# A Mamba block with a dequantized linear layer behind it: the first 512 tokens' x products in two steps of 256 tokens, out_proj's weights turned later

## Chip, cores and metric

The kernel runs on one core of one Trainium2 chip. The metric is the device time of one execution in microseconds, the median of several runs. The core has five engines, each with its own instruction stream: PE (matmul; its weight loads are listed apart as PEld), DVE (vector), ACT (scalar, activation functions), POOL (GpSimd) and SP (here it issues all DMAs). On-chip memory is SBUF (128 partitions) and PSUM (eight banks of 512 float32 a partition), into which PE writes.

## What is computed

For one sequence of L = 4096 tokens of width H = 1024 (float32):

```python
# inner width DIN = 2048, N = 16 states a channel, K = 4 taps, R = 64
def attn(hidden_states):                      # hidden_states = layernorm(x)
    proj = hidden_states @ in_proj_w          # 1024 -> 4096
    x, z = jnp.split(proj, 2, axis=-1)
    xc = conv_b + sum(conv_w[:, k] * shift(x, K - 1 - k))   # causal, along tokens
    xc = silu(xc)
    ssm_p = einsum('bdl,ed->ble', xc, x_proj_w)             # 2048 -> 64 + 16 + 16
    dt_r, Bm, Cm = rmsnorm of its three parts
    dt = softplus(einsum('blr,dr->bdl', dt_r, dt_proj_w) + dt_bias)
    A = -exp(A_log)
    # for every channel d and state n, token after token:
    #   h = exp(dt * A) * h + dt * B * xc ;  y = sum_n h * C
    y = (ys + D_param * xc) * silu(z)
    return einsum('bdl,hd->blh', y, out_proj_w)

x = x + attn(layernorm(x))
x = x + (layernorm(x) @ dequantized_W.T + bias)             # 1024 -> 1024
```

The recurrence over tokens is the scan: its state h carries from token to token, so the token steps go in order.

## The kernel before

**Steps.** Tokens are worked on in chunks of `TC` = 512 (`sizes`, L343), and the scan in steps of `TS` = 256 tokens. DIN is 16 tiles of 128 channels (`ND`), in four groups of four (`NG`). A `block` (L1121) is one scan step of one group; each has two halves (`hf`) of two channel tiles and eight pairs of states (`k`), so that the scan is 64 blocks of 16 units, 1024 units of 2 channel tiles x 2 states x 256 tokens.

**A unit.** `unit_b` (L965) makes `h = u * B` on POOL (L972) and puts the carried state's part into its first column (ACT, L974). `unit_e` (L976) makes `da = exp(dt * A)` on ACT into two PSUM tiles (L984). `unit_s` (L986) scans on DVE (L997), copies the last token's state on ACT into `state` (L1001) and multiplies by C: on DVE (L1003, when the scan's result lies in `da`) or on POOL (L1005, when it lies in `h`); which of the two is chosen unit by unit from the work counted so far. Eight transposes on PE (L1014) then add the products up in the PSUM tile `py`. `unit_b` runs three units ahead (`B_AHEAD`), `unit_e` one (`E_AHEAD`); there are 7 buffers for `h` and 4 for `da`. After eight pairs `py` is copied out (L1192) and `epilogue` (L937) transposes it, multiplies by silu(z), read back from DRAM, and stores y as two parts.

**Matrix products.** Float32 operands are split in a high and a low part, and `product` (L594) makes three matmuls for each of eight 128-row parts of the contraction (L610 to L612), so 24 to a tile. Weights come through `load_wi` (L622): at chunk 0 raw weights are loaded, split on chip, and the split parts stored to DRAM for later; the high half of an x weight is stored at chunk 1 (its low half at chunk 0), and later uses load the split parts (`load_w`). Each tile takes two of the four `w` buffers.

**Stages of a chunk.** `norm_transpose` (L522) normalizes rows and turns them. `gen_x` (L655) makes the 16 x tiles: product, convolution (ACT L685, three steps on DVE L688, last three tokens kept in `halo`, L689), silu (L647, each with a table load before and behind it), store of xc, and behind every four (or two) tiles an `x_proj` (L705, L714). `rms_norms` (L724) and `rms_transpose` (L746) follow; they set the mark `("x", c)`, which the first block of chunk c needs. z tiles come either from `gen_z` (L769, chunk 0) or mixed tile by tile with the x tiles (`mixed`, all later chunks). `prep_group` (L866) makes dt for a block.

**Background.** The scan's loop (L1165) is the backbone. All other work is a generator, `gen_all` (L1086), from which `pull` (L1129) takes a share after each unit: `total * (i + LEAD) / len(units)`. Before the loop it is pulled until the mark `("x", 0)` is there: this is the head of the kernel, without a scan. `side` holds small jobs (turning of weights) that are slipped into the products, `later` delays steps behind a product.

**Order on the engines.** `Order` records every instruction, gives it a rank (its place in the program, less a lead), and `schedule` (L204) replays all of them with a cost for each (`cost`, L161): each engine takes the ready instruction of lowest rank. The order that comes out is fixed with dependencies (`tie`, L304). The chip's engines then run their queues in that order. In the replay any two accesses to one PSUM tile depend on each other.

**Out_proj's weights.** `prep_out_w` (L474) loads out_proj's raw weights, turns them on PE, splits them on ACT and DVE and stores 32 pieces of 512 KB. It is a side job, put in behind `gen_z(0)` (L1088).

Of the kernel before, what the change touches and what calls it, by code (L numbers as in the profile page):

```python
# [16 lines left out]
F32 = mybir.dt.float32  # L17
# [3 lines left out]
ALU = mybir.AluOpType  # L21
# [4 lines left out]
P = 128  # L26
TC = 512
TS = 256
BIG = 1e28
LEAD = 20  # L30
PREP_N = 2
FIRST = 2000
EPI_N = 0
PRE = 3
X_DELAY = 2
# [12 lines left out]
class Order:  # L48
# [112 lines left out]
    def cost(self, r, e, n, silu):  # L161

        op = r.opcode
        if e == 0:
            name = str(r.outs[0])
            if "xps" in name:
                g = 223
            elif "float32r" in str(r.ins[0].dtype):
                g = 6 + 0.434 * n
            else:  # L170
                g = 0.85 * n
            return g, g + 164
        if e == 1:
            if op == "LoadActFuncSet":
                return 1300, 1300
            if op == "TensorCopy":
                d = 170 + 0.815 * n
            else:
                wide = sum(getattr(x, "bass_ap", None) is not None for x in r.ins) > 1
                d = 200 + 1.02 * n if wide else 195 + 0.84 * n  # L180
            if n < 32:
                return 95, 190
            if silu:
                d += 1400
            elif str(r.outs[0].bass_ap.space).endswith("PSUM"):
                return d - 56, d + 17
            return d - 100, d
        if e == 2:
            d = 180 + 2.15 * n
            if op == "TensorTensor" and "pow" in str(r.op):  # L190
                d = 400 + 157 * n
            return d - 40, d
        if e == 3:
            d = 140 + 1.05 * n
            if op == "BNStats":
                d = 676
# [132 lines left out]
def mamba_ffn_kernel(ctx, tc, hs, in_w, conv_w, conv_b, xp_w, dt_w, dt_b, a_log, d_par, out_w,  # L329
# [10 lines left out]
    NG = ND // 4  # L340
    NHB = H // P
    NTS = TS // P
    sizes = [TC] * (L // TC)  # L343
    osizes = [TC] * (L // TC - 1) + [TS] * 2
    starts = [sum(sizes[:i]) for i in range(len(sizes))]
    ostarts = [sum(osizes[:i]) for i in range(len(osizes))]
# [27 lines left out]
    def dense(name):  # L374
        return ps_d.tile([P, TC], F32, tag="dense", name=name)
# [175 lines left out]
    def start(kind, c):  # L551

        assert kind == "x" or writes[id(x1b_s[c])] == NHB
        src = hs[starts[c]:starts[c] + sizes[c], :] if kind == "x" else x1b_s[c]
        it = norm_transpose(src)
        norms[kind, c] = (next(it), it)
        side.insert(0, [1, itertools.islice(it, PRE)])
# [33 lines left out]
        while later:  # L591
            yield later.pop(0)[1]()

    def product(ps, w, act):  # L594

        for k in range(KT):
            if k == 4:
                for e in later:
                    e[0] -= 1
                for e in [e for e in later if e[0] <= 0]:  # L600
                    later.remove(e)
                    yield e[1]()
            if k == 2 and side:
                for _ in range(side[0][0]):
                    yield from side_step()
            while len(act) < KT:
                yield next(norm_it[id(act)])
            hi, lo = act[k]
            wk = w[k // 4]
            nc.tensor.matmul(ps, wk[:, 0, k % 4, :], hi, start=(k == 0), stop=False)  # L610
            nc.tensor.matmul(ps, wk[:, 0, k % 4, :], lo, start=False, stop=False)  # L611
            nc.tensor.matmul(ps, wk[:, 1, k % 4, :], hi, start=False, stop=(k == KT - 1))  # L612
            yield 3 * MM * hi.shape[-1] / TC
# [38 lines left out]
    ctx_c = [dict() for _ in range(NCH)]  # L652
    done_marks = set()

    def gen_x(c, mixed, nxt=None):  # L655

        t0, sz = starts[c], sizes[c]
        nt = sz // P
        act = yield from finish("x", c)
        ctx_c[c]["xn"] = act  # L660
        ssm = smp.tile([P, TC // P, E], F32, tag="ssm", name="ssm", bufs=1)[:, :nt]
        corr = smp.tile([P, ND, 3], F32, tag="corr", name="corr", bufs=1)
        part = smp.tile([P, ND, 3], F32, tag="part", name="part", bufs=1)
# [6 lines left out]
        for p in range(ND // nx):  # L670
# [3 lines left out]
            for i in range(4):  # L674
                j = i // 2 if mixed else i
                m = p * nx + j
                if mixed and i % 2:
                    yield from z_tile(c, m, act, pre[:, nx + j, :])
                    continue
                w = load_wi(c, m)  # L680
                ps = dense("ips")[:, :sz]
                yield from product(ps, w, act)
                with tc.high_priority(1000):
                    t = pre[:, j, :]
                    nc.scalar.activation(t, ps, AF.Identity, scale=cw[:, m, 3:4], bias=cb[:, m:m + 1])  # L685
                    for k in (2, 1, 0):
                        o = t[:, 3 - k:]
                        nc.vector.scalar_tensor_tensor(o, ps[:, 0:sz - 3 + k], cw[:, m, k:k + 1], o, ALU.mult, ALU.add)  # L688
                    nc.scalar.copy(halo[:, m, :], ps[:, sz - 3:sz])  # L689
# [4 lines left out]
            if mixed:  # L694
                nc.sync.dma_start(sz_s[c][g][:, h:h + nx, :], pre[:, nx:, :])
                done_marks.add(("z", c, g, h))
            later.append([(X_DELAY if p < ND // nx - 1 else X_DELAY_LAST) if c else 1, partial(first, c, x_proj, c, p * nx, nx, pre, ssm)])
        later.append([X_DELAY_LAST if c else 1, partial(first, c, rms_norms, c, ssm)])

    def first(c, f, *args):  # L700
# [65 lines left out]
        done_marks.add(("x", c))  # L766
        return 2 * nt * TP

    def gen_z(c):  # L769
        act = ctx_c[c].pop("xn")  # L770
        sz = sizes[c]
        for g in range(NG):
            pre = prep.tile([P, 4, TC], F32, tag="pre", name="prez")[:, :, :sz]
            for j in range(4):
                yield from z_tile(c, g * 4 + j, act, pre[:, j, :])
            silu(pre)
            nc.sync.dma_start(sz_s[c][g], pre)
            done_marks.add(("z", c, g, 2))

    def z_tile(c, m, act, dst):  # L780
        w = load_wi(c, ND + m)
        ps = dense("zps")[:, :sizes[c]]
        yield from product(ps, w, act)
        with tc.high_priority(1000):
            nc.scalar.copy(dst, ps)
# [200 lines left out]
    def unit_s(v, py):  # L986
# [7 lines left out]
        for n in range(2):  # L994
            flat = da[n].rearrange("p a b -> p (a b)")
            hflat = h[:, n].rearrange("p a b -> p (a b)")
            nc.vector.tensor_tensor_scan(hflat if on_pool else flat, flat, hflat, 0.0, ALU.mult, ALU.add)  # L997
        for n in range(2):
            last = (h[:, n] if on_pool else da[n])[:, :, TS - 1]
            if not (c == NCH - 1 and s == sizes[c] // TS - 1):  # L1000
                nc.scalar.copy(state[:, g0:g0 + 2, 2 * k + n], last)  # L1001
            if not on_pool:
                nc.vector.tensor_tensor(h[:, n], da[n], cb_[:, n], ALU.mult)  # L1003
        if on_pool:
            nc.gpsimd.tensor_tensor(h, h, cb_, ALU.mult)  # L1005
        hc = h
        terms = [(n, hc[:, n]) for n in range(2)]
        if k == 0:
# [220 lines left out]
```

## Time and profile before

| | |
|---|---|
| median of 3 runs | 4419.52 us (4413.35 to 4423.57) |
| profiled execution | 4422.55 us, span 4420.8 us |
| mean granted TensorE clock | 0.968 |
| DMA | 1066.39 MB, mean 241 GB/s |
| scans (L997) | 2048: 1166 into da, 882 into h |
| exps of da (L984) | 4096, 473 ns each, 1858.6 us |
| first multiply by B on POOL (L972) | 1024, 2388 ns each, 2423.9 us |
| multiply by C on POOL (L1005) | 441, 2396 ns each, 1055.4 us |
| state copies on ACT (L1001) | 1098 from da of 160 ns, 822 from h of 188 ns |
| table loads on ACT (L647, L648) | 64 and 64, 1283 ns each |
| out_proj's weights turned | 285 to 504 us |

How to read it: the busy time of an engine is the sum of the stretches in which it had an instruction at work; busy PE also holds pipelined matmuls whose ends are modelled. A line such as "ACT x <- DVE y: 10, 5, 3" in the list of waits says that ACT stood idle 10 us in all, 5 times, at most 3 us, ahead of x until DVE had done y. Each engine works off its own queue in order, so a wait holds up what is queued behind it. The chain of waits follows the work that ended last back to the start, and names at each step what it was released by.

### The profile page before, as it was taken

To read this page: it belongs to the slowest core of one execution; us is meant where nothing else is said; L and a number is where in the kernel's file an instruction comes from. 1 tells how busy PE (TensorE), PEld (TensorE's weight loads), DVE (VectorE), ACT (ScalarE), POOL (GpSimd) and SP (SyncE) were. 2 spreads that over 40 slices of the span, in tenths; PEclk is the share of its full clock that TensorE was granted. 3 is DMA by queue.
4 is the path that set the end of the run, shared out by engine and by line. 5 is a ranking of instruction groups with operands and counts; after the bars stand their busy time and mean duration, and the time that the engine had idled before them with its cause. 6 is when DMAs were issued, how large, how long until landed. Compare 5 with 4: busy or idle time off the path is not lost.

```text
span 4420.8 us, 73712 instructions
## 1 busy us (share of the span) xinstructions
PE 4072.3 (92%) x23658; PEld 3451.4 (78%) x23658; DVE 3908.0 (88%) x4842; ACT 3573.4 (81%) x9854; POOL 3853.4 (87%) x2234
## 2 busy tenths in 40 slices
PE   8988899999988999999999999999999999998887
PEld 6767778777876887788777888788877878887776
DVE  5588889998999989999899999999989999998882
ACT  5788888888887888888888789888888877877671
POOL 0678799899997999999999999999998999999791
PEclk9989999999999999999999999999999999999987
DMA  8868866567678765987568875788566898988765
GB/s 261 270 226 286 289 215 217 178 201 222 187 249 273 238 216 174 298 263 246 180 209 272 254 255 184 250 277 277 189 200 215 302 320 264 308 256 275 241 223 189
DMA packets 693843, 1066.39 MB, mean 241 GB/s; under 512 B 63816, under 2 KB 488832, under 8 KB 692432
## 3 DMA queue, kind: packets, MB, share of 16 engines
q1 hardware_dynamic: 693456, 1061.68, 74.1%
q8 instruction: 187, 3.06, 0.3%
q14 instruction: 200, 1.64, 0.1%
HBM read 815.85 MB, written 245.63 MB: 240 GB/s over the span
## 4 chain that ended last, share of the span: by engine, by line
PE 47%; ACT 13%; POOL 13%; DVE 10%; DMA 8%; issue 4%; SPq 1%; DVEq 0%; POOLq 0%; ACTq 0%
PE py L1014 11%; POOL h L972 7%; ACT da L984 4%; DVE da L997 4%; POOL h L1005 4%; PE ops L610 3%; PE ops L611 3%; PE ops L612 3%; PE ips L610 3%; PE ips L612 3%; PE ips L611 3%; PE zps L610 2%; PE zps L611 2%; PE zps L612 2%; DVE h L1003 2%
## 5 line engine op out<-in xcount | busy, mean ns | idle before, releaser
L972 POOL TENSOR_TENSOR h<-xl,bb 128x1020 f32<-128x1020 f32 x1024 | 2423.9, 2388 | 214.7 <-PE py L1014 201.5
L984 ACT ACTIVATE da<-dt,amat 128x256 f32<-128x256 f32 x4096 | 1858.6, 473 | 186.0 <-DVE h L1003 143.4
L997 DVE TENSOR_TENSOR_SCAN da<-da,h 128x512 f32<-128x512 f32 x1166 | 1378.4, 1213 | 66.0 <-POOL h L972 26.5
L1014 PE MATMUL py<-ident,h 128*128 128x128 f32 x8192 | 1116.6, 280 | 97.9 <-POOL h L1005 73.7
L1014 PEld LDWEIGHTS py<-ident,h 128*128 128x128 f32 x8192 | 972.2, 144 | 219.2 <-POOL h L1005 103.1
L1005 POOL TENSOR_TENSOR h<-h,cc 128x1024 f32<-128x1024 f32 x441 | 1055.4, 2396 | 80.8 <-ACT state L1001 71.6
L997 DVE TENSOR_TENSOR_SCAN h<-da,h 128x512 f32<-128x512 f32 x882 | 1044.9, 1208 | 44.4 <-ACT da L984 32.5
L1003 DVE TENSOR_TENSOR h<-da,cc 128x512 f32<-128x512 f32 x1166 | 755.4, 677 | 49.0 <-ACT state L1001 48.0
L610 PE MATMUL ops<-yh,wt 128*128 128x512 f32 (+1 forms) x1152 | 457.2, 398 | 19.5 <-DMA yh<-y 5.8
L611 PE MATMUL ops<-yh,wt 128*128 128x512 f32 (+1 forms) x1152 | 431.4, 375 | 2.4 <-DMA yh<-y 2.2
L612 PE MATMUL ops<-yh,wt 128*128 128x512 f32 (+1 forms) x1152 | 431.0, 374 | 0.0
L610 PE MATMUL zps<-nh,wt 128*128 128x512 f32 x896 | 365.9, 408 | 6.9 <-DVE nh L409 2.8
L612 PE MATMUL zps<-nh,wt 128*128 128x512 f32 x896 | 358.4, 400 | 0.0
L611 PE MATMUL zps<-nh,wt 128*128 128x512 f32 x896 | 357.9, 399 | 0.0
L610 PE MATMUL ips<-nh,wt 128*128 128x512 f32 x768 | 316.1, 412 | 20.2 <-DVE ssm L721 8.4
L688 DVE SCALAR_TENSOR_TENSOR pre<-ips,cw,pre 128x511 f32<-128x511 f32 (+2 forms) x384 | 281.3, 733 | 48.6 <-ACT pre L685 41.6
L612 PE MATMUL ips<-nh,wt 128*128 128x512 f32 x768 | 307.2, 400 | 0.0
L611 PE MATMUL ips<-nh,wt 128*128 128x512 f32 x768 | 306.7, 399 | 0.0
L1001 ACT COPY state<-da 128x2 f32<-128x2 f32 x1098 | 158.8, 160 | 150.0 <-DVE da L997 144.5
L610 PEld LDWEIGHTS ops<-yh,wt 128*128 128x128 f32 x1152 | 223.0, 194 | 53.0 <-DVE xb L835 7.7
L612 PEld LDWEIGHTS ops<-yh,wt 128*128 128x128 f32 x1152 | 222.0, 193 | 36.4
L611 PEld LDWEIGHTS ops<-yh,wt 128*128 128x128 f32 x1152 | 223.6, 194 | 30.8 <-DMA yh<-y 4.7
(163 smaller groups left out, 7159.3 us busy)
## 6 DMA issues: line engine op xcount, KB each, us to landing
wt<-wi SPq DMA_DIRECT2D x416, 512.0 KB, 4.3
wt<-wo SPq DMA_DIRECT2D x288, 512.0 KB, 5.3
wt<-wf SPq DMA_DIRECT2D x144, 512.0 KB, 4.8
yh<-y SPq DMA_DIRECT2D x224, 256.0 KB, 6.2
xl<-xc SPq DMA_DIRECT2D x64, 512.0 KB, 6.3
bb<-b SPq DMA_DIRECT2D x128, 256.0 KB, 5.8
cc<-b SPq DMA_DIRECT2D x128, 256.0 KB, 6.4
ze<-sz SPq DMA_DIRECT2D x128, 256.0 KB, 4.2
```

The lines of the kernel that those rows point to most:

```text
L610: nc.tensor.matmul(ps, wk[:, 0, k % 4, :], hi, start=(k == 0), stop=False)
L611: nc.tensor.matmul(ps, wk[:, 0, k % 4, :], lo, start=False, stop=False)
L612: nc.tensor.matmul(ps, wk[:, 1, k % 4, :], hi, start=False, stop=(k == KT - 1))
L688: nc.vector.scalar_tensor_tensor(o, ps[:, 0:sz - 3 + k], cw[:, m, k:k + 1], o, ALU.mult, ALU.add)
L972: nc.gpsimd.tensor_tensor(h[:, :, :, 1:], u[:, js, 1:].unsqueeze(1).to_broadcast([P, 2, 2, TS - 1]), bb[:, :, 1:].unsqueeze(2).to_broadcas ...
L984: nc.scalar.activation(da[n][:, j, :], dt[:, 2 * hf + j, :], AF.Exp, scale=amat[:, d, 2 * k + n:2 * k + n + 1])
L997: nc.vector.tensor_tensor_scan(hflat if on_pool else flat, flat, hflat, 0.0, ALU.mult, ALU.add)
L1001: nc.scalar.copy(state[:, g0:g0 + 2, 2 * k + n], last)
L1003: nc.vector.tensor_tensor(h[:, n], da[n], cb_[:, n], ALU.mult)
L1005: nc.gpsimd.tensor_tensor(h, h, cb_, ALU.mult)
L1014: nc.tensor.matmul(py[:, i * P:(i + 1) * P], src[:, j, tb * P:(tb + 1) * P], ident, is_transpose=True, start=(n < 0 and i == 0), stop=(k = ...
```

## The change

The first chunk of 512 tokens is cut in two of 256 (`sizes`), both normalized and transposed at once; the x products, convolution, x_proj and norms are made for the first 256 tokens, then the mark `("x", 0)` is set. The z products of those 512 tokens stay 512 wide; their group 0 comes first, then chunk 1's x tiles, with z group 1 between the two halves of them, then z groups 2 and 3. The next chunk (512 tokens; it was chunk 1 and is now chunk 2) has its x tiles first and its z tiles behind them, no more mixed (`APART`). `prep_out_w` is put in at chunk 3, the second chunk of 512. In `unit_s`, a unit whose product with C is on POOL makes one state copy for its two states in place of two; where it is on DVE, each state's multiply comes before its copy. The planner's costs for matmuls are raised.

```diff
+APART = 2
...
             if "xps" in name:
-                g = 223
+                g = 234
             elif "float32r" in str(r.ins[0].dtype):
-                g = 6 + 0.434 * n
+                g = 10 + 0.45 * n
             else:
-                g = 0.85 * n
+                g = 0.9 * n
...
-    sizes = [TC] * (L // TC)
+    sizes = [TS] * 2 + [TC] * (L // TC - 1)
...
-        src = hs[starts[c]:starts[c] + sizes[c], :] if kind == "x" else x1b_s[c]
+        src = hs[starts[c]:starts[c] + max(sizes[c], TC), :] if kind == "x" else x1b_s[c]
...
-    def product(ps, w, act):
+    def product(ps, w, act, cs=slice(None)):
...
-            hi, lo = act[k]
+            hi, lo = act[k][0][:, cs], act[k][1][:, cs]
...
-    def gen_x(c, mixed, nxt=None):
+    def gen_x(c, mixed, nxt=None, between=None):
...
-        act = yield from finish("x", c)
-        ctx_c[c]["xn"] = act
+        if c == 1:
+            act = ctx_c[0]["xn"]
+        else:
+            act = ctx_c[c]["xn"] = yield from finish("x", c)
+        cs = slice(c * TS, c * TS + TS) if c < 2 else slice(None)
...
-                yield from product(ps, w, act)
+                yield from product(ps, w, act, cs)
...
+            if between and p == ND // nx // 2 - 1:
+                yield from between
...
-    def gen_z(c):
-        act = ctx_c[c].pop("xn")
-        sz = sizes[c]
-        for g in range(NG):
-            pre = prep.tile([P, 4, TC], F32, tag="pre", name="prez")[:, :, :sz]
-            for j in range(4):
-                yield from z_tile(c, g * 4 + j, act, pre[:, j, :])
-            silu(pre)
-            nc.sync.dma_start(sz_s[c][g], pre)
-            done_marks.add(("z", c, g, 2))
+    def gen_z(c, g):
+
+        pre = prep.tile([P, 4, TC], F32, tag="pre", name="prez")
+        for j in range(4):
+            yield from z_tile(c, g * 4 + j, ctx_c[c]["xn"], pre[:, j, :])
+        silu(pre)
+        for i in range(TC // sizes[c]):
+            nc.sync.dma_start(sz_s[c + i][g], pre[:, :, i * sizes[c]:(i + 1) * sizes[c]])
+            done_marks.add(("z", c + i, g, 2))
...
-        for n in range(2):
-            last = (h[:, n] if on_pool else da[n])[:, :, TS - 1]
-            if not (c == NCH - 1 and s == sizes[c] // TS - 1):
-                nc.scalar.copy(state[:, g0:g0 + 2, 2 * k + n], last)
-            if not on_pool:
+        keep = not (c == NCH - 1 and s == sizes[c] // TS - 1)
+        st = state[:, g0:g0 + 2, 2 * k:2 * k + 2]
+        if on_pool:
+            if keep:
+                nc.scalar.copy(st.rearrange("p j n -> p n j"), h[:, :, :, TS - 1])
+            nc.gpsimd.tensor_tensor(h, h, cb_, ALU.mult)
+        else:
+            for n in range(2):
                 nc.vector.tensor_tensor(h[:, n], da[n], cb_[:, n], ALU.mult)
-        if on_pool:
-            nc.gpsimd.tensor_tensor(h, h, cb_, ALU.mult)
+                if keep:
+                    nc.scalar.copy(st[:, :, n], da[n][:, :, TS - 1])
...
     def gen_all():
-        yield from gen_z(0)
-        side.append([1, prep_out_w()])
+        yield from gen_z(0, 0)
+        yield from gen_x(1, False, None, gen_z(0, 1))
+        for g in range(2, NG):
+            yield from gen_z(0, g)
         o = f = 0
-        for c in range(1, NCH):
-            yield from gen_x(c, True, ("f", f) if f < o else None)
+        for c in range(2, NCH):
+            if c == 3:
+                side.append([1, prep_out_w()])
+            yield from gen_x(c, c > APART, ("f", f) if f < o else None)
+            if c <= APART:
+                for g in range(NG):
+                    yield from gen_z(c, g)
```

More of the change, by code (lines that the diff above doesn't have):

```diff
@@ L767, in rms_transpose @@
         return 2 * nt * TP
-    def gen_z(c):
-        act = ctx_c[c].pop("xn")
-        sz = sizes[c]
-        for g in range(NG):
-            pre = prep.tile([P, 4, TC], F32, tag="pre", name="prez")[:, :, :sz]
-            for j in range(4):
-                yield from z_tile(c, g * 4 + j, act, pre[:, j, :])
-            silu(pre)
-            nc.sync.dma_start(sz_s[c][g], pre)
-            done_marks.add(("z", c, g, 2))
+    def gen_z(c, g):
[6 more added lines that the diff above has]
+            done_marks.add(("z", c + i, g, 2))
     def z_tile(c, m, act, dst):
         w = load_wi(c, ND + m)
-        ps = dense("zps")[:, :sizes[c]]
+        ps = dense("zps")[:, :dst.shape[-1]]
         yield from product(ps, w, act)
```

## The prediction

> **What bounds the kernel now.** I read the page's first two parts, then stages of the span, then the instructions around the first scan, then the chain of waits and the list of waits.
>
> The page (busy time of each engine, then tenths in 40 slices of 110.5 us):
>
> ```profile
> span 4420.8 us, 73712 instructions
> PE 4072.3 (92%) x23658; PEld 3451.4 (78%) x23658; DVE 3908.0 (88%) x4842; ACT 3573.4 (81%) x9854; POOL 3853.4 (87%) x2234
> DVE  5588889998999989999899999999989999998882
> POOL 0678799899997999999999999999998999999791
> ```
>
> Three engines are near full together; only at the head and in the tail do DVE and POOL stand idle. Stages (length, then busy us of PE, PEld, DVE, ACT, POOL, granted clock, DMA share, GB/s):
>
> ```profile
> 26.00:133.00 107.00, 105.24 (x519) 87.45 (x520) 57.55 (x87) 53.14 (x89) 4.50 (x6) 1.00 0.78 245
> ...
> 300.00:600.00 300.00, 263.10 (x1500) 220.98 (x1500) 261.29 (x318) 257.06 (x692) 245.98 (x132) 0.95 0.81 271
> 600.00:1800.00 1200.00, 1104.37 (x6298) 928.83 (x6298) 1087.08 (x1336) 1021.53 (x2798) 1095.05 (x637) 0.97 0.68 218
> 1800.00:4000.00 2200.00, 2104.21 (x12261) 1779.53 (x12259) 2080.15 (x2539) 1850.01 (x5317) 2088.84 (x1173) 0.99 0.77 250
> ```
>
> In the head (26 to 133 us) PE is full with the x products of 512 tokens while POOL does nothing. Later PE, DVE and POOL share the bound: from 1800 to 4000 us they are 95.6%, 94.6% and 94.9% busy. So an earlier scan relieves DVE and POOL, but whatever PE no longer does in the head it must do later. The first scan and its releaser, from the timelines of DVE and POOL (start, us):
>
> ```profile
> 133.48 2.32 DVE L688 SCALAR_TENSOR_TENSOR pre<-ips,cw,pre 128x511 f32<-128x511 f32 x3 [3.12 <-ACT pre L685]
> ...
> 173.58 3.45 DVE L997 TENSOR_TENSOR_SCAN da<-da,h 128x512 f32<-128x512 f32 x3
> ```
> ```profile
> 170.15 2.37 POOL L972 TENSOR_TENSOR h<-xl,bb 128x1020 f32<-128x1020 f32 x1
> ```
>
> The last product of the first chunk ends near 132.7 us, the first scan starts at 173.6: 41 us of dependent steps lie between. Then the chain by engine, and the waits around the copies of the state (us, times, longest):
>
> ```profile
> PE 47%; ACT 13%; POOL 13%; DVE 10%; DMA 8%; issue 4%; SPq 1%; DVEq 0%; POOLq 0%; ACTq 0%
> ```
> ```profile
> ACT state L1001 <- DVE da L997: 144.5, 197, 3.2
> ACT da L984 <- DVE h L1003: 143.4, 251, 3.7
> ...
> POOL h L1005 <- ACT state L1001: 71.6, 51, 5.9
> ...
> DVE h L1003 <- ACT state L1001: 48.0, 51, 4.1
> ```
>
> **Term A, the head.** 16 tiles of 24 products. Between starts of neighbouring matmuls the timeline shows 0.2275 us at 512 columns (138 to 148 us) and 0.12 us at 256 columns at full clock (4338 to 4344 us). 384 x 0.2275 = 87.4 us becomes 384 x 0.12 = 46.1. Three of the four x_proj groups lie inside the head, 3.7 us each, and halve: 11.1 becomes 5.6. Turning the small weights (4 us) and the cold start (2 us) stay. 104.5 becomes 57.7: 47 less if PE alone sets the pace. The stage must also move its data: per tile 0.5 MB in and 0.5 MB out, with the norm rows, small weights and xc some 23 MB before the last product, which at 283 GB/s (mean of the first 60 us, 229, 292 and 327) takes 81 us against 26 + 58 = 84 on PE. So nearly a tie; I put the last product at 90 instead of 132.7: 43 less. Of the 41 us behind it, a halved last x_proj saves 1.9 us, two of four groups of dd and bc 1.4, half of the power at L734 (2.3 us) about 1: 4 us. **A = -47**, bounds -30 (a tile every 4.2 us, as one store of a weight tile takes 4.4 us to land) and -51.
>
> **Term B, what goes under the scan.** Chunk 1's products, 46.1 us, and its x_proj, 7.4 us, now run on PE beside the scan: 53.5 us. How much is path is not to be seen directly: nothing if PE always had a gap, all if PE is the bound. I take PE's share of the chain, 47%: +25. DVE gets 48 convolution steps of 0.47 us (the 256-column row of L923), 22.7 us, at its 10%: +2. ACT gets 16 evacuations of 0.47, 16 halo copies of 0.16, and four more silu groups: the old one is load 1.28, silu 1.92, load 1.28, and a half silu is about 1.0, so 3.6 each; 7.5 + 2.6 + 14.3 = 24 us at 13%: +3. POOL gets 1.3 us of corr and a second power: under 1. **B = +31**, bounds +5 and +60.
>
> In this trace a silu follows its table load at once, and the next work the second load: load at 110.98 us, silu at 112.27, load at 114.21, next at 115.50. The Trainium skill, "ScalarE: Activation LUTs", section "What ACT_TABLE_LOAD costs", counts about 1.38 us of drain on top of 1.283 us for each table switch, which speaks against the change. By it eight more loads would be an estimated 21 us of ACT rather than 10.3, and the sum about 1.4 us longer; no such drain is seen here.
>
> Queues: chunk 1's raw weights, low halves and stored high halves are the five DMAs a tile that the old chunk 1 issued. New on SP's queue are 32 loads of 512 KB for chunk 2 (16.8 MB beside 1066), four more stores of sz and four of xc, some eight loads of xw and those of the second norm: about 50 issues of 0.4 us, 20 us on a queue that mostly waits for landings. They cost nothing while SP issues ahead; without that cover they are in the slower rival. On POOL's queue 11 of the 32 splits of the z weights (L409, 1.29 us) lay before the first scan; now only group 0's 8 do, and three, 4 us, join the scan's work: under 1 us at POOL's 13%.
>
> **Term C, the state copies.** On the POOL path 822 copies (188 ns) become 411 of 128x4, priced by the 128x4 copy at L974 (197 ns): 155 - 81 = 74 us less on ACT, at 13%: -10. On the DVE path the multiply no longer queues behind the copy: the 48.0 us wait goes, at DVE's 10%: -5. In exchange the copy is the last reader of da, so an exp that waited for the multiply (251 times) now waits for a 0.16 us copy too: 40 us at 13%, +5. Behind a waiting copy on ACT stand the next exps, and behind those the scan. POOL's 71.6 us wait stays: its multiply still needs a copy after the second scan. **C = -10**, bounds -58 (all of DVE's wait and the 10) and +30 (all 40, less the 10).
>
> **Term D, out_proj's weights turned in chunk 3.** They are turned from 285 to 504 us now. From 300 to 600 us 67 units of the scan start (first multiply on POOL, L972: 22, 25, 20 per 100 us), against 24.3 per 100 us from 600 to 1800: 6 units, 24 us, are lost. The 16 raw loads and 32 stores on SP's queue (24 MB) move from DMA shares of 0.79 to 0.84 to shares of 0.61 to 0.67, but PE, ACT and DVE do the same turning there. I take half: **D = -12**, bounds -24 and +10.
>
> **Term E.** The planner's higher matmul costs (240 instead of 228 ns for 512 columns; the row says 0.2275 at full clock) and chunk 2 with x before z change only the order of issue. No row prices that: 0, bounds -15 and +15.
>
> Sum: -47 + 31 - 10 - 12 = -38. The profiled execution took 4422.55 us (span 4420.8); it lies 3.0 above the median of the runs, 4419.52. 4422.6 - 38 - 3 = 4382; I take **4383 us**.
>
> Splitting 384 products costs 2 x 46.1 - 87.4 = 4.8 us of PE by the rows. The Trainium skill, "TensorE: Matmul & The Clock Gate", section "Back-to-back issue gap", gives N/2.4 + 2.5 ns for an isolated matmul and warns that it under-counts at small N. By it 256 columns would take an estimated 109 ns, against 120 here, and the split would cost 1 us; no other number rests on it.
>
> **Rivals.** 1) **PE is the whole bound.** For it: PE is fullest, and 98% busy in the head already, so the early scan buys no PE time. Against it: 96 us of PE idle from 600 to 1800 and as much from 1800 to 4000. B = +60, D = 0: -47 + 60 - 10 = +3, less 3: 4423, no change.
> 2) **The scan's engines are the bound.** For it: DVE and POOL were idle exactly in the head. B = +5, C = -20, D = -24: -86: 4334. Against it: PE's 47% of the chain.
> 3) **Chunk 1's weights come late (slower).** A tile moves three 0.5 MB pieces, 1.57 MB; at 277 GB/s, the rate from 300 to 560 us, that is 5.7 us per tile, where PE needs 2.9 + 0.5. PE runs its queue in order, so the transposes of the scan (L1014) stand behind a product that waits, POOL waits for its h buffers (the wait of 201.5 us in the list), and 16 x 2.3 = 37 us go lost. It decides if DMA stays over 0.95 from the first scan to the last product of chunk 1 and PE is the bound as in rival 1: +3 + 37 = +40, 4460. Against: z tiles (5.5 us on PE) lie between the halves.
> 4) **The scan doesn't begin earlier**, because something else of the head (the dt weights, the table loads) is late too: A near 0 leaves 31 - 10 - 12 = +9: 4429. Against: the dt weights are stored by 84 us and would come sooner with the products.
>
> **How the numbers follow.** Chances: forecast 0.45 (its own range 4362 to 4408), rival 1 0.16, rival 2 0.16, rival 3 0.20, rival 4 0.03. A measurement of this kernel tells about 0.2% from no change, 9 us: 4411 to 4428. Faster is forecast and rival 2, 0.60 (a little of the forecast runs over); same is rival 1, 0.16; slower is rivals 3 and 4 and a little of 1, 0.24. The range reaches to rival 2 with A at its bound, 4328, and just over rival 4, 4435, leaving out most of rival 3 and a little below.
>
> **What would show it.** First scan (L997) at 122 to 133 us; products of ips with 256 columns every 0.12 us; PE's busy time up by about 5 us, DVE's by 10 (48 steps of 2 x 0.47 for 0.74); copies at L1001 from 1920 to some 1510, the wait of L1003 on them near zero; units in the first 600 us up from 98 to 115 or more; a rate from 1800 to 4000 us a little under today's 26 per 100 us. Wrong would be a first scan after 145 us, PE waiting on wi from DMA for more than 30 us before 350 us, or waits on owt as long in chunk 3 as they are now.

## The result, and the profile after

The changed kernel took 4457.19 us, the median of 4 runs (4455.44 to 4464.32), beside 4421.55 us for the kernel before: a ratio of 1.0084, 95% interval 1.0069 to 1.0100. It is 36 us slower. The forecast was 4383, with a range up to 4435. Its profiled execution took 4464.32 us, the longest of the four.

The page of the kernel after, as it was shown of the one before (span and busy time, then tenths in 40 slices):

```profile
span 4462.5 us, 74483 instructions
PE 4102.5 (92%) x24042; PEld 3464.6 (78%) x24042; DVE 3906.7 (88%) x4886; ACT 3545.1 (79%) x9486; POOL 3866.5 (87%) x2247
DVE  5689888988989999999899988899988999998772
POOL 0679989889997999899999989999998989999771
```

POOL reaches 9 in the fourth slice (before in the sixth), and in the last three slices both engines have lower digits (772 and 771, before 882 and 791). The stages (length, busy us of PE, PEld, DVE, ACT, POOL, granted clock, DMA share, GB/s):

```profile
200.00:300.00 100.00, 90.44 (x572) 79.48 (x571) 80.92 (x113) 91.09 (x230) 73.13 (x51) 0.98 0.94 308
300.00:600.00 300.00, 280.84 (x1599) 235.28 (x1598) 267.97 (x338) 259.69 (x675) 278.08 (x175) 0.97 0.64 210
600.00:1800.00 1200.00, 1109.45 (x6380) 926.42 (x6379) 1093.59 (x1342) 1016.42 (x2685) 1098.25 (x617) 0.98 0.71 237
1800.00:4000.00 2200.00, 2103.47 (x12110) 1756.72 (x12109) 2033.81 (x2486) 1792.49 (x4961) 2043.96 (x1152) 0.99 0.76 248
```

From 300 to 600 us POOL does 32 us more than before (278 to 246), which is what the change was made for. From 1800 to 4000 us it does 45 us less (2044 to 2089) and DVE 46 us less, while PE is as full as it was (2103 to 2104). The first scan, in DVE's timeline (start, us):

```profile
143.35 0.69 DVE L935 TENSOR_TENSOR dt<-dt,dps 128x512 f32<-128x512 f32 x1 [2.20 <-ACT dps L933]
150.21 2.35 DVE L1002 TENSOR_TENSOR_SCAN da<-da,h 128x512 f32<-128x512 f32 x2 [6.17 <-ACT h L979]
```

It starts at 150.2 us, 23.4 us sooner than the 173.6 of before, not 47. POOL's first multiply starts 31.4 us sooner (138.79 after 170.15); the scan then waits 6.2 us for ACT. The first dt is finished earlier still, at 135.7 us; the 37 us in an expectation below are not those of DVE's row. The waits around the state copies and y (us, times, longest):

```profile
ACT state L1013 <- DVE h L1011: 224.5, 236, 2.7
...
POOL h L1008 <- ACT state L1007: 105.5, 77, 6.7
...
ACT da L989 <- DVE h L1002: 81.9, 114, 3.0
PEld yps L423 <- ACT yhi L422: 79.9, 94, 3.7
...
DVE h L1002 <- ACT da L989: 57.4, 27, 4.8
...
ACT da L989 <- DVE h L1011: 33.8, 23, 3.7
```

DVE's wait for the copies (48.0 us before) is gone. The wait of ACT's copies of da has grown from 144.5 to 224.5 us, but most of that has only moved: the exps, which waited 143.4 us for the multiply, now wait 33.8 for it and 81.9 for a scan (16.7 before). With the copies of h (29.6, now 19.1) these four waits of ACT are 334 us before and 359 after. The wait of POOL for a copy has grown from 71.6 to 105.5, that of the scans for exps from 32.5 to 57.4, and PE's for the high part of y from 23.9 to 79.9.

How far the scan has come is the best gauge for all runs. This table counts units of the scan up to a time (POOL's busy time in the first multiply, divided by 2.387 us); 24 to 26 are done in 100 us, so one is worth some 4 us. The last five kernels are explained below.

```
us             200  300  400  600  800  1800  3400  4300
before           7   30   51   94  140   378   783  1010
after           16   33   53  103  150   387   783   999
split only      16   33   52   96  134   376   774   997
lag only        11   37   59  104  135   373   774   995
new head        15   33   52   98  145   381   782  1006
head + copies   16   36   54  103  148   382   784  1008
head + costs    14   31   53  102  148   380   779   999
```

The kernel after is 9 to 10 units ahead from 600 to 1800 us, has lost them all by 3400, and is 11 behind at 4300, some 45 us.

### The profile page after: what moved, and what is told of

Its sections match the earlier page's. It is cut to its first block, busy times and chain, and to the rows that moved or that the text cites. A ratio compares the mean times of both kernels' runs of the same rounds, so it can differ in the third digit from the quotient of the medians.

```text
span 4462.5 us, 74483 instructions
## 1 busy us (share of the span) xinstructions
PE 4102.5 (92%) x24042; PEld 3464.6 (78%) x24042; DVE 3906.7 (88%) x4886; ACT 3545.1 (79%) x9486; POOL 3866.5 (87%) x2247
## 5 line engine op out<-in xcount | busy, mean ns | idle before, releaser
L977 POOL TENSOR_TENSOR h<-xl,bb 128x1020 f32<-128x1020 f32 x1024 | 2424.5, 2387 | 210.9 <-PE py L1022 194.8
L989 ACT ACTIVATE da<-dt,amat 128x256 f32<-128x256 f32 x4096 | 1840.3, 474 | 141.4 <-DVE h L1002 81.9
L1008 POOL TENSOR_TENSOR h<-h,cc 128x1024 f32<-128x1024 f32 x445 | 1064.3, 2394 | 112.6 <-ACT state L1007 105.5
L1002 DVE TENSOR_TENSOR_SCAN h<-da,h 128x512 f32<-128x512 f32 x890 | 1047.6, 1209 | 98.9 <-ACT da L989 57.4
L611 PE MATMUL ips<-nh,wt 128*128 128x512 f32 x896 | 372.0, 415 | 15.3 <-DMA wt<-wi 11.8
L613 PE MATMUL ips<-nh,wt 128*128 128x512 f32 x896 | 354.5, 396 | 0.0
L612 PE MATMUL ips<-nh,wt 128*128 128x512 f32 x896 | 353.8, 395 | 0.0
L1013 ACT COPY state<-da 128x2 f32<-128x2 f32 x1088 | 162.3, 160 | 228.0 <-DVE h L1011 224.5
L692 DVE SCALAR_TENSOR_TENSOR pre<-ips,cw,pre 128x509 f32<-128x509 f32 (+5 forms) x432 | 291.9, 676 | 42.6 <-ACT pre L689 39.0
```

Source lines behind the costliest of these rows:

```text
L977: nc.gpsimd.tensor_tensor(h[:, :, :, 1:], u[:, js, 1:].unsqueeze(1).to_broadcast([P, 2, 2, TS - 1]), bb[:, :, 1:].unsqueeze(2).to_broadcas ...
L989: nc.scalar.activation(da[n][:, j, :], dt[:, 2 * hf + j, :], AF.Exp, scale=amat[:, d, 2 * k + n:2 * k + n + 1])
L1013: nc.scalar.copy(st[:, :, n], da[n][:, :, TS - 1])
```

## The experiments

Each ratio is taken against runs of the kernel before on the same chip (medians 4419.70 to 4421.73). "Before" and "after" name the two kernels.

**How steady is a time against a mere change of order?** In null_order a cost of the planner is changed by 0.001 ns an element, which changes nothing but the order of some instructions.

```diff
-                g = 6 + 0.434 * n
+                g = 6 + 0.435 * n
```

> The kernel before with one planner cost changed by 0.2% (6 + 0.435 n for 6 + 0.434 n): no work, no stage changes, only ties in the order may fall the other way. It shows how far chance in the order alone moves the time. If order is chance of 0.3%: anywhere from 4406 to 4433 us. If the order is steady: 4415 to 4425 us.

Measured 4417.57 us, ratio 0.9992 (0.9981 to 1.0003), no difference from before. Differences of some 4 us between kernels of different order are given no cause below.

**The parts alone.** u_only is before with the new state copies, c_only before with the new matmul costs, h_only before with the new head (the split, chunk 2's x ahead of its z, out_proj's weights late), and no_u the head with the costs, so after without the new copies.

> The kernel before with the state copies of the change alone. Theory U (a copy behind the multiply keeps da longer, exps come late and the scan waits for them): 4435 to 4455 us, DVE's idle time for exps of da about 100 us instead of 49. Theory H (the head and what it moves under the scan is the cause): 4405 to 4425 us, no slower than before. Theory C (the planner's new matmul costs): 4405 to 4425 us.

> The kernel before with the planner's three matmul costs of the change alone. Theory C: 4435 us or more. Theories U and H: 4405 to 4435 us, only the order of issue differs.

> The kernel before with the split first chunk, chunk 2 with x before z, and out_proj's weights turned at chunk 3, but the old state copies and the old costs. Theory H: 4440 us or more. Theory U: the early scan (37 us sooner) pays back at least a part, 4385 to 4415 us. Theory C: the same.

> The changed kernel with the old state copies. Theory U: 4395 to 4430 us, the loss of 36 us gone. Theory H: 4445 to 4465 us. Theory C: 4445 to 4465 us.

Measured: u_only 4429.89, ratio 1.0022 (1.0011 to 1.0032); c_only 4423.33, 1.0005 (0.9995 to 1.0014); h_only 4431.02, 1.0027 (1.0016 to 1.0038); no_u 4470.05, 1.0114 (1.0097 to 1.0132). No part alone is faster. The costs are worth 2 us by themselves and 39 beside the new head. no_c completes it, the head with the copies at the old costs, and half_c is no_u with costs half way.

```diff
-                g = 10 + 0.45 * n
+                g = 6 + 0.434 * n      # no_c, and 223 and 0.85 * n
+                g = 8 + 0.442 * n      # half_c, and 228 and 0.875 * n
```

> The changed kernel with the old matmul costs in the planner. If the parts simply add, before + copies (10) + head (11): 4440 us. If the new costs and the new head make the loss together (head with new costs, old copies: 50 over before; head alone 11; costs alone 2), it is 4415 to 4430 us.

> The new head with the old copies and matmul costs halfway between old and new (228 for xps, 8 + 0.442 n, 0.875 n). With the old costs it took 4431 us, with the new ones 4470. If the costs act steadily: 4445 to 4455 us. If a small change of cost only reshuffles the order by chance, it can land anywhere, also outside 4431 to 4470.

Measured: no_c 4427.07, ratio 1.0013 (1.0004 to 1.0022); half_c 4445.75, 1.0059 (1.0044 to 1.0074). Beside the new head and the old copies the costs act steadily: 4431, 4446, 4470. With the new copies they cost 30 us (4427 to 4457). That is most of the loss. With the costs PE stands longer for ACT's high part of y. From 1800 to 4000 us, of c_only:

```profile
PEld yps L422 <- ACT yhi L421: 36.7, 55, 2.2
```

of no_u:

```profile
PEld yps L423 <- ACT yhi L422: 38.0, 57, 2.7
```

and of h_only, with the old costs:

```profile
PEld yps L423 <- ACT yhi L422: 5.0, 16, 0.6
```

The planner now takes PE to be slower (240 ns for 512 columns, measured 228), so it lets ACT come to y later than PE is there. But c_only has the same wait and loses nothing by it. The wait shows that the order is off; that it is the way the 30 to 39 us are lost is not shown.

**Is PE the bound?** In before_less the products of the low half of the weights are left out in the x tiles of chunks 1 and 2, in after_less in those of chunks 2 and 3, and in before_late in those of chunks 5 and 6: 256 products of 0.2275 us, 58 us of PE, with the pace of the background kept.

```diff
-            nc.tensor.matmul(ps, wk[:, 1, k % 4, :], hi, start=False, stop=(k == KT - 1))
+            if not two:
+                nc.tensor.matmul(ps, wk[:, 1, k % 4, :], hi, start=False, stop=(k == KT - 1))
...
-                yield from product(ps, w, act)
+                yield from product(ps, w, act, c in (1, 2))
```

> The kernel before without the products of the weights' low half in the x tiles of chunks 1 and 2: 256 matmuls of 512 columns, 58 us of PE, left out of the scan's time (the output lacks that part of x); loads, pacing and all else stay. It prices PE work under the scan. PE is the bound: 58 us or nearly that less, 4360 to 4370 us. PE's share of the chain, 47%: 4390 us. The scan's engines are the bound: 4410 to 4420 us.

> The changed kernel without the same products of the same tokens (chunks 2 and 3 there), 58 us of PE left out. PE is the bound: 4395 to 4405 us, so below the kernel before: the 53 us that the head hands to PE are then what eats the early scan. At 47%: 4430 us. The scan's engines or the order of issue: 4445 to 4460 us.

> The kernel before without the products of the weights' low half in the x tiles of chunks 5 and 6: again 256 matmuls, 58 us of PE left out (the output lacks that part of x), but in the stretch from some 2000 to 2900 us, where PE is 96% busy. If PE is the bound there and was not at 300 to 600 us: 4360 to 4385 us. If PE is the bound nowhere: 4410 to 4425 us, as with chunks 1 and 2.

Measured: before_less 4422.82, ratio 1.0009 (0.9998 to 1.0021); after_less 4465.4, 1.0099 (1.0075 to 1.0123), where after has 1.0084; before_late 4424.1, 1.0005 (0.9992 to 1.0018). In three places 58 us less of PE saved nothing. From 1800 to 3400 us, before and then before_late:

```profile
1800.00:3400.00 1600.00, 1527.59 (x8900) 1288.94 (x8898) 1509.84 (x1848) 1373.00 (x3894) 1521.48 (x865) 0.99 0.73 236
```
```profile
1800.00:3400.00 1600.00, 1490.72 (x8565) 1260.24 (x8564) 1502.40 (x1836) 1366.32 (x3872) 1510.93 (x862) 0.96 0.72 235
```

With 335 fewer matmuls in this stretch (256 are left out of the kernel) PE is busy only 37 us less, and the granted clock fell from 0.99 to 0.96; DVE and POOL did a little less than before, not more.

**The split alone.** h_split has the split at the old costs and with the old copies, but chunk 2 mixed as it was, and out_proj's weights put in with that chunk. Against h_only:

```diff
-APART = 2
+APART = 1
...
-            if c == 3:
+            if c == 2:
                 side.append([1, prep_out_w()])
```

> The split first chunk alone, with old copies and costs; chunk 2 mixed and out_proj's weights turned in that chunk, as in the kernel before. If the split itself costs what the head gains: 4425 to 4440 us, as the whole new head with old costs (4431). If turning the weights at chunk 3 or the unmixed chunk 2 was the loss: 4385 to 4415 us.

Measured 4468.5, ratio 1.0117 (1.0096 to 1.0139): the split alone costs 47 us, and chunk 2's x ahead of z and the later weights give 37 of them back. The loss has one striking place, though not all of it lies there. POOL's first multiplies (L977) come every 4 us in the mean, but from 724 to 773 us there are 49 us in which none starts. The stretch in h_split:

```profile
725.00:750.00 25.00, 23.12 (x112) 19.04 (x111) 19.86 (x33) 14.95 (x41) 12.36 (x17) 1.00 0.60 186
750.00:775.00 25.00, 22.50 (x122) 18.64 (x121) 7.23 (x12) 17.08 (x27) 3.25 (x4) 0.93 0.72 245
```

PE is 92% and 90% busy, POOL stands. The same stretch of before:

```profile
725.00:750.00 25.00, 23.13 (x142) 19.60 (x141) 23.26 (x28) 22.79 (x61) 24.04 (x20) 1.00 0.85 268
750.00:775.00 25.00, 25.00 (x137) 21.03 (x136) 20.05 (x23) 22.54 (x56) 25.00 (x12) 1.00 0.80 260
```

Counted from 0, unit 128 is the first of tokens 512 on (two steps of 64 units). It needs their dt, which begins with `rr` in `rms_transpose`; POOL's `xl` (L894, L889 in before) uses that dt once for each block. The loop has a line for it: at the third pair of the block ahead, `pull(until=("x", c + 1))` takes all the background that is still missing. In h_split, from DVE's, POOL's and PE's timelines:

```profile
753.80 0.69 DVE L762 TENSOR_TENSOR rr<-rps,hf 64x512 fp32r<-64x512 f32 x1 [7.95 <-ACT hf L761]
...
772.85 0.69 DVE L935 TENSOR_TENSOR dt<-dt,dps 128x512 f32<-128x512 f32 x1 [1.56 <-ACT dps L933]
```
```profile
772.81 2.37 POOL L977 TENSOR_TENSOR h<-xl,bb 128x1020 f32<-128x1020 f32 x1 [15.78 <-PE py L1019]
...
775.39 2.37 POOL L894 TENSOR_TENSOR xl<-dt,xl 128x1024 f32<-128x1024 f32 x1
...
778.42 2.38 POOL L977 TENSOR_TENSOR h<-xl,bb 128x1020 f32<-128x1020 f32 x1
```
```profile
712.57 0.82 PE L1019 MATMUL py<-ident,h 128*128 128x128 f32 x6
...
770.90 0.66 PE L1019 MATMUL py<-ident,xd 128*128 128x128 f32 x4
```

The multiply at 772.81 is still one of the tokens before: it waits for PE, which does none of the scan's transposes between 713 and 771 us but mostly products. Tokens 512 on follow behind it: their dt is finished at 773.5 us, `xl` comes at 775.39, the first multiply at 778.42. So two waits lie on each other, one for PE, which is busy with products, and one for dt.

In before this `rr` comes at 694.7 us and the longest pause there is 12 us:

```profile
726.87 2.38 POOL L889 TENSOR_TENSOR xl<-dt,xl 128x1024 f32<-128x1024 f32 x1
```

That is 32 us behind `rr`, where 22 are enough in h_split, so some 10 us are to spare. In h_only `rr` comes at 574.0, in no_c at 559.3 and in after at 558.1. So the scan has a due time: tokens 512 on, when 128 units are done. The split starts the scan sooner, so the due time is sooner, and puts 53.5 us of products in front of those tokens. h_split misses it; the others take 16 z tiles and the turning out of the way, and meet it.

**Lag alone.** If that is so, before must lose as much when nothing is split and only the background comes 52 us later at the start, the same work made up evenly until the end.

```diff
-        pull(total * min(1.0, (i + LEAD) / len(units)))
+        pull(total * min(1.0, 1.0217 * (i + LEAD) / len(units) - 0.0217))
```

> The kernel before with the background drawn as the split draws it: 52 us of planned work later against the scan at the start, with the lag made up evenly until the end (the scan gets 2.2% more background per unit). No work is changed and the first scan comes no sooner. If the lag of the background is what eats the early scan: 4445 to 4475 us. If not: 4412 to 4430 us.

Measured 4471.89, ratio 1.0117 (1.0102 to 1.0132), the same as h_split. `rr` of tokens 512 on comes at 751.6 us, the pause there is 52 us, and up to it the scan ran ahead (104 units at 600 us, before 94). Its row:

```profile
750.00:775.00 25.00, 22.38 (x141) 19.67 (x142) 10.75 (x16) 14.65 (x32) 6.60 (x7) 0.93 0.72 243
```

So lag alone is enough for such a loss. How it adds up is seen by when POOL's `xl` of the same block starts, against before (us, - is sooner; times of before in the first row):

```
                 block 5  block 8  block 19  block 63
before             520.2    726.9    1476.9    4246.6
h_split            -18.1    +48.5     +10.0     +48.6
before_lag         -29.9    +44.0      +9.3     +52.5
h_only             -14.3    -17.6     -14.6      +7.8
no_c               -27.8    -34.7     -24.7      +2.9
outw_late          -29.6    -17.0     -11.1      -5.5
d_only             -25.1    -31.1     -27.7     -26.0
```

Block 8 is the first of tokens 512 on. After the pause most of the delay is caught up by block 19; some 40 us of h_split's and before_lag's loss come bit by bit behind it. Each row is one profiled execution; those of outw_late (4416.0 us) and d_only (4404.6), which are explained below, are the slowest and the fastest of theirs.

The other way round, no_c_pace draws the background 6% sooner than no_c.

```diff
-        pull(total * min(1.0, (i + LEAD) / len(units)))
+        pull(total * min(1.0, 1.06 * (i + LEAD) / len(units)))
```

> The changed kernel with the old matmul costs (4427 us) and background work drawn 6% earlier against the scan, so that less of PE's work is left for the stretch from 1800 us on, where PE is 96% busy. If the density of PE work there eats the early scan: 4395 to 4415 us. If not: 4420 to 4440 us.

Measured 4546.26, ratio 1.0286 (1.0267 to 1.0305), far off what was expected. The background ran ahead, took the scan's time, and then had nothing to do until the scan gave it y. From 3400 to 4300 us PE is busy 742 of 900 us (before 832):

```profile
3400.00:4300.00 900.00, 742.40 (x4217) 637.81 (x4217) 749.77 (x914) 617.53 (x1750) 744.79 (x414) 0.90 0.68 220
```

Of the two other paces that were tried, the later one lost 50 us (on before) and the earlier one 119 (on no_c).

**Do late weights set it?** no_lo is no_c without the loads of the low halves of chunk 1's x weights (8.4 MB) and their products.

```diff
-                nc.sync.dma_start(w[q][:, 1].bitcast(F32), wi_s[m][q][:, 1])
...
-                yield from product(ps, w, act, cs)
+                yield from product(ps, w, act, cs, c in (1,))
```

> The changed kernel with the old costs (4427 us), in chunk 1's x tiles without the loads of the weights' low halves (8.4 MB less in the stretch where DMA is 0.94 busy) and without their products (15 us of PE; the output lacks that part of x). If late weights in that stretch eat the lead of the scan and a lead kept is worth its time at the end: 4395 to 4412 us. If a lead gained there is lost later in any case: 4420 to 4430 us.

Measured 4426.48, ratio 1.0012 (1.0001 to 1.0023), as no_c (4427.07). The stretch that was feared is in the kernel after, with a DMA share of 0.94 from 200 to 300 us and 17 units where before did 23; and the scan loses lead there: after is 40 us ahead at POOL's `xl` of the second block (178.0 us, before 217.8) and 7 at the third (278.3, before 285.2). But that is made up, 34 us ahead at 622 us; and in no_lo, with less to move, the fourth block comes 25 us ahead, where it is 12 in no_c, and the end does not come sooner.

**Order of the first chunks without the split.** outw_late is before with out_proj's weights put in one chunk later; d_only has chunk 1's x ahead of its z besides.

```diff
         yield from gen_z(0)
-        side.append([1, prep_out_w()])
         o = f = 0
         for c in range(1, NCH):
+            if c == 2:
+                side.append([1, prep_out_w()])
-            yield from gen_x(c, True, ("f", f) if f < o else None)
+            yield from gen_x(c, c > 1, ("f", f) if f < o else None)  # d_only
+            if c == 1:                                               # d_only
+                yield from gen_z(c)                                  # d_only
```

> The kernel before with out_proj's weights turned one chunk later and nothing else. Theory of the prediction's term D (half of 24 us back): 4400 to 4415 us. If the turning costs the same wherever it lies: 4415 to 4430 us.

> The kernel before with one chunk of 512 in the head as it was, but its second chunk with x before z and out_proj's weights turned in the third. Beside the split these two were worth 37 us (4468 without them, 4431 with them). If they are worth that without the split too: 4380 to 4400 us. If they only repaired what the split spoils: 4412 to 4428 us.

Measured: outw_late 4402.97, ratio 0.9956 (0.9942 to 0.9970); d_only 4410.52, 0.9970 (0.9961 to 0.9980). Of all kernels with the whole computation, outw_late has the lowest median, below both that were given. There `rr` of tokens 512 on comes at 673.9 us, 20.8 before the time of before. In d_only it comes at 491.1, and that gives no more at the end: so much sooner than due was worth nothing here.

**One chain or two?** scan_less is before without the multiply by C in 64 units of chunks 3 and 4 (154 us of DVE and POOL, some 77 each); both_less leaves out, besides, what before_late left out on PE in the same stretch.

```diff
-        on_pool = order.load[2] + POOL_MORE < order.load[3]
+        skip = c in (3, 4) and k in (3, 7)
+        on_pool = skip or order.load[2] + POOL_MORE < order.load[3]
...
-        if on_pool:
+        if on_pool and not skip:
```

> The kernel before, with the multiply by C left out in 64 of the 1024 units (pairs 3 and 7 of the scan's chunks 3 and 4, at some 1820 to 2830 us); everything else is kept. 64 x 2.4 = 154 us less work for POOL and DVE, some 77 us for each. Theory of two chains of nearly equal length (the scan's on DVE and POOL, the background's on PE), each waiting for the other at places fixed in the program: 4400 to 4422, at most a fifth of the 77 us, because the background doesn't get shorter. If the scan's engines alone set the end: 4345 to 4370.

> As the run before (the multiply by C left out in 64 units at 1820 to 2830 us), and besides, as in the run before_late, without the products of the low half of the weights in the x tiles of chunks 5 and 6, 58 us less of PE in the same stretch, which alone gave nothing (4424). Theory of two chains: shortened together they give nearly the smaller of the two, so 4360 to 4385. If the scan's engines alone set the end: the same time as the run before, both at 4345 to 4370. If something third holds the kernel (the order of the steps, or a transfer): both within 10 us of the kernel before, 4410 to 4430.

Measured: scan_less 4396.45, ratio 0.9938 (0.9918 to 0.9958); both_less 4386.99, 0.9920 (0.9895 to 0.9945). Neither theory has its number. 77 us less for the scan's engines gave 25, a third; with PE's 58 besides it was 34, and as the intervals overlap the 9 more are not certain. From 1800 to 2900 us, scan_less:

```profile
1800.00:2900.00 1100.00, 1072.01 (x6321) 912.26 (x6319) 1023.78 (x1231) 973.05 (x2770) 1031.43 (x595) 0.99 0.77 248
```

PE is busy 21 us more than before here (1050.75) and does 185 more matmuls: as soon as the scan's engines have less to do, PE takes up the slack and is at 97.5%. So neither side is the bound alone, and two chains of quite the same length are too simple a picture as well.

## Why the prediction was wrong

By parts, each the step between two measured kernels: the split +47 (before to h_split), chunk 2's x first and the weights later -37 (to h_only), the copies -4 (to no_c), the costs +30 (to after). The sum is +36. Forecast for the same steps were -16 (A and B), -12 (D, and chunk 2's order at nothing), -10 and 0, so the errors are +63, -25, +6 and +30.

**Term A, the head, was -47 and is -23** by the first scan, -31 by POOL's first multiply. The last x product of the first chunk ends at 113.9 us and not at 90 (before 132.7). The part behind it held: from there to the first scan it takes 36.3 us, 4.6 less than before, where 4 were forecast; a silu of z with its table loads, which lies in ACT's queue ahead of the first column of h in both kernels, now holds DVE 6.2 us. What failed is the "nearly a tie" of transfers and PE. The 23 MB were counted from the start of the kernel, but 6.16 MB move up to 26 us and 24.05 MB from 26 to 114 us, 30 in all. From 26 to 96 us:

```profile
26.00:96.00 70.00, 53.79 (x355) 50.42 (x356) 36.71 (x69) 33.90 (x65) 0.42 (x2) 0.86 0.99 303
```

The DMA share is 0.99; PE is busy 54 of 70 us and gets a clock of 0.86 (before 1.00 from 26 to 133 us). With products half as long most of the head is bound by its weights. Its end is not: from 96 to 114 us the DMA share is 0.44 and PE is busy 16.1 of 18 us, at a clock of 0.89. PE's busy time from 26 to 114 us is 69.9 us, where 58 were forecast at full clock. The lower bound of the term, -30, was too strong.

**Term B, the work moved under the scan, failed, and most.** It was priced by PE's share of the chain of waits, 47% of 53.5 us, and so was +31 with an upper bound of +60. h_split costs 47 us although its first scan comes 27 us sooner (146.1 us), so there B is about +74. That share is no price: 58 us less of PE saved nothing, three times, and 53.5 us more in front of tokens that had some 10 us to spare stopped the scan for 49 us. The step should have asked when the tokens behind the moved products are needed: at unit 128. h_split and before_lag show it, with pauses of 49 and 52 us just ahead of that unit. The pause is not the whole price, as the blocks show: by block 19 the two are 10 and 9 us behind, and 39 and 43 more are lost until the last block. The DVE and POOL shares, 10% and 13%, were too small in turn: 77 us less on both would be 18 us by them, and gave 25.

**Term C, the copies, was -10.** It is +10 alone (u_only), -4 beside the new head (too little to tell from nothing) and -13 beside head and costs, inside the bounds of -58 and +30. DVE's wait vanished as said. ACT's wait for the multiply moved from the exps to the copies, and the four waits grew by 25 us in all. That POOL's wait stays was wrong (71.6 to 105.5).

**Term D, the weights turned later, was -12.** The sign is right and the size too small: -19 in outw_late, with bounds of -24 and +10. What it is worth beside the split, where it lies in front of the due tokens, was not measured by itself; together with chunk 2's order it is 37.

**Term E, the planner's costs and chunk 2's order, was 0 with bounds of 15, and is +30 to +39 for the costs beside the new head.** "Change only the order of issue" was true and no reason for a small bound: a change of order may cost 30 us where everything is close. The order of chunk 2, put at nothing in the same sentence, gives 37 us back beside the split, together with term D.

**The rivals.** PE as the whole bound (4423) falls with before_less and before_late. The scan's engines as the bound (4334) falls with the result, and scan_less gave a third of what it demanded. Late weights (4460) had nearly the right time by luck: its stretch is in the trace, and in it the scan loses 33 us of its lead, but they are made up later, and no_lo took weights away and nothing came of it. That the scan doesn't begin earlier is wrong. Of the signs that were named, units in the first 600 us (9 more by the table, 17 forecast) were off and pointed to A; the 98 there counts a multiply that crosses from one 100 us into the next twice, and is 94 by the table. PE's busy time rose by 30 us (4072.3 to 4102.5), not 5, and DVE's not at all. The first scan after 145 us was named as a sign of error, and came.

**What stays open.** With the old costs and the tokens in time (no_c, h_only) the kernel is ahead by 8 and 5 units at 800 us and behind by 2 and 4 at 4300. It loses 9 to 10 units, some 40 us, in 3500 us, and before_lag loses as many after its pause, h_split 7. All four have some 53 us more background left under the scan. By the blocks they lose 22 to 43 us from block 19 to the last, outw_late and d_only, which have no more background than before, 6 and 2. That the background is what costs them is argued from this and not shown: the three runs with 58 us less on PE speak against a simple form of it. How the raised costs lose 30 us beside that head, and 2 without it, is also open.

## What to carry to other kernels

Where a first stage is cut so that a consumer starts sooner, work out when the consumer will need the next piece, and what stands in front of that piece: where it came too late the consumer stood for 49 us here, and where it came in time (h_only, no_c) the moved work was still not free, as the kernels end 11 and 7 us behind before. An engine's share of the chain of waits is not the price of work on it; leaving some out shows the price, and may show zero on an engine that is 96% busy. Change the costs of a planner in a run of its own, beside the order that it is to be used with.

## What was not expected of the hardware

Taking products away lowered PE's clock. In all ten runs of before_late its mean is 0.959 to 0.965, where before has 0.965 to 0.970; in before_less it is 0.959 to 0.964, beside 0.967 to 0.971. In before_late 335 matmuls fewer from 1800 to 3400 us left the mean busy time of one at 174.0 ns, where it was 171.6 (1490.72 us by 8565, 1527.59 by 8900), with the granted clock at 0.96 and 0.99. In the head of the kernel after, from 60 to 100 us, PE was busy 30.0 of 40 us at a granted clock of 0.79, where before it was busy 39.8 at 1.00. So a PE that waits for data is here also slower when the data is there.

The Trainium skill, "TensorE: Matmul & The Clock Gate", section "Part 1: The HAM clock gate", says that a gate sets PE's clock by how busy PE has recently been, half or full. The two stretches agree with that in direction, and the lower step can be seen in the kernel after:

```profile
106.50:110.00 3.50, 3.50 (x18) 3.50 (x19) 2.41 (x5) 0.78 (x2) 0.19 (x1) 0.52 0.49 183
```

From 106.7 to 109.9 us the x products of 256 columns start 0.21 us apart, from 110.1 us on 0.12. The clocks in between, such as 0.79, are means over longer stretches.
